# A graph-attention layer on one core: the order of a step, copies between lanes in place of matmuls, and early query blocks behind the table

## Chip, cores and metric

One Trainium2 chip, one of its cores. The metric is the device time of one execution in microseconds, as the median of several runs; lower is better. A profile holds one execution, with its span from the first to the last instruction. Engines: PE (matrix multiply, with PEld for its weight loads), DVE (vector), ACT (scalar functions), POOL (here: indirect loads), SP (issues loads and stores). Each works through its own queue in order, and waits on semaphores for the others.

## What is computed

A graph-attention layer over 3125 nodes of 128 features (8 heads of 16) and 100,000 edges sorted by destination, each with one of 5 relations, followed by two layer norms. Cut to what matters:

```python
for r in range(R):                                  # 5 relations
    mask = edge_types == r
    q = einsum('eh,khd->ekd', x[dst], W_Q[r])
    k = einsum('eh,khd->ekd', x[src], W_K[r])
    v = einsum('eh,khd->ekd', x[src], W_V[r])
    logits = (q * k).sum(-1) / scale + attn_bias[r]
    max_v = segment_max(where(mask, logits, NEG), dst)
    exp_l = where(mask, exp(logits - max_v[dst]), 0)
    attn = exp_l / (segment_sum(exp_l, dst)[dst] + 1e-12)
    out = out + segment_sum(attn * v, dst)
h = out.reshape(n, 128) @ out_proj_w.T + out_proj_b + x
y = (h - mean(h)) / sqrt(var(h) + eps) * ln_gamma + ln_beta
result = layernorm(x + y)
```

## The kernel before

**Start.** Inputs are loaded; W_K, W_V and W_Q are turned on PE (`wp`). A loop over 25 blocks of 128 nodes (`turn`, `table`, L318 to L341) turns a block of x, multiplies it with all W_K and W_V and stores the product to `kv_d` in DRAM: a table with one row of k and v for each node and relation. Beside it DVE makes keys, masks and indices (`side`). Then ACT issues the loads of beta, gamma, out_w, the bias (`floor`) and out_b (`lift`), and the pools of this stage (`load`, `pps`, `work`) are closed; their memory goes to the main pools (`ps`, `flow`, and the kv tiles 3 to 5).

**Queries.** A block of queries (`turn_q`, `turned`, `queries`, `first_part`, `remainder`, `second_part`, `third_part`, `store_q`) is x times W_Q, split into three bf16 parts whose sum is the f32 value, and stored to `q_d` in DRAM. `queries` makes it in two halves, of 3 and 2 relations. Blocks 0 to 3 are made before the main loop, each with its own load of x; the others inside it: `q_from` gives the step at which block b begins (q0); its second half follows one step later (q1), its last part and its store another step later (q2).

**Main loop.** The edges are cut into 196 groups of 512, and a step k has three groups: 66 steps, and a few more to drain. Each step issues, in an order written out by hand (the tile framework keeps this order on each engine), pieces of several groups of three:
- `fetch(k+3)` on SP: edge keys `kt`, query rows `qw`, masks `mk`. `gather` on POOL, up to three steps ahead: 12 indirect loads of table rows to one of six `kv` buffers.
- `spot(k+2)` on DVE and `spread_q(k+1)` on PE: the query of each edge (`qe`, in PSUM).
- `logits(k)` on DVE (three instructions, L632 to L635); `turn_logits` on PE, to lanes: one partition for each of group, relation and head, 120 in all, 512 edges along it; `keep_logits` on ACT.
- `scans(k)` on DVE: a running maximum forward and one back, restarted where the destination changes. So each lane has the maximum of every destination within its group of 512. A destination may straddle two groups: `joins` brings each lane the last value of the lane 40 before it, and the first value of the lane 40 behind it (40 lanes to a group; over the border of a step from and to the neighbouring step's tile `m`). Before, this is a product with a shifted unit matrix on PE, from `shift`, to a PSUM tile `c`; it runs for step k-1, as it needs m of step k.
- `less_max(k-2)` on DVE takes c into account and subtracts the maximum; `exps(k-2)` on ACT; `turn_exps(k-2)` on PE turns back; `weights(k-2)` (ACT) and `weigh(k-2)` (DVE) multiply with v. `weigh` is the last reader of a kv buffer.
- `places` (k-2) on ACT: a one-hot matrix for each group; `sums` (k-3) on PE adds up by destination; `carry` (ACT) hands a group's last destination to the next group.
- `norm(k-3)`, `relations(k-3)`, `by_node(k-4)`: division, sum over relations, copy to `oT`.
- For a block whose edges are all done (`done_at`): `project` on PE, one step later `residual` (DVE) and `norms` (a square root on ACT, then DVE), two steps after that `store_z`.

Of the kernel before, what the change touches and what calls it, by code (L numbers as in the profile page):

```python
# [8 lines left out]
F32 = mybir.dt.float32  # L9
BF16 = mybir.dt.bfloat16  # L10
# [107 lines left out]
def windowed_path(  # L118
# [15 lines left out]
    def keep(name, shape, dt=F32):  # L134
        return const.tile(shape, dt, name=name)
# [24 lines left out]
    work = pre.enter_context(tc.tile_pool(name="work", bufs=2))  # L160


    full = (NT - 1) * P
    xn = load.tile([P, NT, H], F32, name="xn")
    nc.vector.memset(xn[:, NT - 1, :], 0.0)
# [56 lines left out]
    base = load.tile([HG, 2], I32, name="base")  # L222


    ident = keep("ident", [P, P])
    make_identity(nc, ident)

    def iota(name, pattern, n, base=0, mult=0, dt=F32, pool=const):
        t = pool.tile([P, n], dt, name=name)
        nc.gpsimd.iota(  # L230
            t, pattern=pattern, base=base, channel_multiplier=mult,
            allow_small_or_imprecise_dtypes=True,
        )
        return t
# [4 lines left out]
    relf = iota("relf", [[1, R]], R, pool=load)  # L239
    nrel = iota("nrel", [[-1, R]], R, pool=load)  # L240
    lane = iota("lane", [[LANES, G3], [HEADS, R], [1, HEADS]], L3, mult=-1, pool=load)
    far = iota("far", [[1, 8 * LANES]], 8 * LANES, base=-L3, mult=-1, pool=load)
    eps_t = keep("eps_t", [P, 1])
    nc.vector.memset(eps_t, LN_EPS)
    ones = keep("ones", [P, P])
# [58 lines left out]
            op=ALU.is_equal,  # L304
        )

    shift = keep("shift", [P, 8 * LANES])
    gather_heads = keep("gather_heads", [P, G3, HEADS])

    def lanes():  # L310
        nc.vector.tensor_scalar(shift, far, 0.0, None, op0=ALU.is_equal)
        nc.vector.tensor_scalar(lane, lane, 0.0, None, op0=ALU.is_equal)
        nc.vector.tensor_reduce(
            gather_heads, lane.rearrange("p (i r k) -> p i k r", r=R, k=HEADS), AX.X, ALU.add
        )
# [163 lines left out]
    for b in range(NT):  # L479
# [3 lines left out]
        for f in side.get(b, ()):  # L483
            f()


    nc.scalar.dma_start(beta_t, beta.partition_broadcast(P))
    nc.scalar.dma_start(gamma_t, gamma.partition_broadcast(P))
# [20 lines left out]
    def groups(k):  # L509
        return range(k * G3, min(NGR, (k + 1) * G3)) if 0 <= k < NST else ()  # L510
# [45 lines left out]
    def first_part(b, c0):  # L556
        pr, q3, n = live["pr", b, c0]
        nc.scalar.copy(q3[:, :, 0, :], pr)
# [112 lines left out]

    def joins(k):
        n = len(groups(k)) * LANES
        c = ps.tile([L3, 2], F32, name="c", tag="small")
        m = live["m", k]
        left = [(m[:n, GE - 1 : GE], shift[:n, 2 * LANES : 2 * LANES + n])]
        if k:
            p = live["m", k - 1]
            left.append((p[:, GE - 1 : GE], shift[:L3, 5 * LANES : 5 * LANES + n]))
        right = [(m[:n, 0:1], shift[:n, 4 * LANES : 4 * LANES + n])]  # L680
        if k + 1 < NST:
            a, an = live["m", k + 1], len(groups(k + 1)) * LANES
            right.append((a[:an, 0:1], shift[:an, LANES : LANES + n]))
        for s, parts in enumerate((left, right)):
            for j, (col, w) in enumerate(parts):
                nc.tensor.matmul(  # L686
                    c[:n, s : s + 1], w, col, start=(j == 0), stop=(j == len(parts) - 1)
                )
        live["c", k] = c

    def less_max(k):
        n = len(groups(k)) * LANES
# [115 lines left out]
    def residual(b):  # L808
# [8 lines left out]
        moments(live["mv", b][:, 0, :], h[:n], n)  # L817
        live["h", b] = h

    def norms(b):  # L820
        mv = live.pop(("mv", b))
        sd = flow.tile([P, 2], F32, name="sd")
        nc.scalar.activation(sd, mv[:, :, 1], AF.Sqrt, bias=eps_t, scale=1.0)  # L823
        nc.vector.reciprocal(sd, sd)
        if b < NT:
            n = min(P, N - b * P)
            h = live.pop(("h", b))
            nc.vector.scalar_tensor_tensor(
                h[:n], h[:n], mv[:n, 0, 0:1], gamma_t[:n], op0=ALU.subtract, op1=ALU.mult
            )  # L830
            y = flow.tile([P, H], F32, name="y")
            nc.vector.scalar_tensor_tensor(
                y[:n], h[:n], sd[:n, 0:1], live.pop(("xr", b))[:n], op0=ALU.mult, op1=ALU.add
            )
            if ("mv", b + 1) not in live:
                live["mv", b + 1] = pair()
# [19 lines left out]
    for b in range(1, NT):  # L856
        done_at[b] = max(done_at[b], done_at[b - 1] + 1)
    done_at[NT] = done_at[NT - 1] + 1


    q_from = []
    for b in range(NT):
        need = min(g for g in range(NGR) if min(block_of(g) + 1, NT - 1) >= b) // G3
        q_from.append(need - 6)
    for b in range(NT - 2, -1, -1):
        if q_from[b + 1] > 0:
            q_from[b] = min(q_from[b], q_from[b + 1] - 2)

    first_b = [b for b in range(NT) if q_from[b] < 1]
    gathered = -1  # L870
    for gathered in range(KVA):
        gather(gathered)
    for b in first_b:
        fetch_x("xq", b)
        turn_q(b)
        turned(b)
        for c0, c1 in ((0, RH), (RH, R)):
            queries(b, c0, c1)
            first_part(b, c0)
            remainder(b, c0)  # L880
            second_part(b, c0)
            third_part(b, c0)
        store_q(b)
    for k in range(3):
        fetch(k)
    spot(0)
    spread_q(0)
    spot(1)
    for k in range(done_at[NT] + 3):
        q0 = next((b for b in range(NT) if q_from[b] == k and b not in first_b), None)  # L890
        q1 = next((b for b in range(NT) if q_from[b] == k - 1 and b not in first_b), None)
        q2 = next((b for b in range(NT) if q_from[b] == k - 2 and b not in first_b), None)

        if k + 3 < NST:
            fetch(k + 3)
        for b in range(NT):
            if q_from[b] == k + 1 and b not in first_b:
                fetch_x("xq", b)
            if done_at[b] == k:
                fetch_x("xr", b)  # L900
            if done_at[b + 1] + 2 == k:
                store_z(b)
# [5 lines left out]
        for b in range(NT):  # L908
            if done_at[b] + 1 == k:
                residual(b)  # L910
        if groups(k - 2):
            less_max(k - 2)
            exps(k - 2)
        if groups(k - 4):
            by_node(k - 4)
        if q0 is not None:
            turn_q(q0)
            turned(q0)
        if q1 is not None:
            queries(q1, RH, R)  # L920
            first_part(q1, RH)
        if q2 is not None:
            third_part(q2, RH)
            store_q(q2)

        sum_g = list(groups(k - 3))
        place_g = list(groups(k - 2))

        def sum_next():
            if sum_g:  # L930
                g = sum_g.pop(0)
                sums(g)
                carry(g)

        def place_next():
            if place_g:
                places(place_g.pop(0))

        sum_next()
        if groups(k):  # L940
            logits(k)
        if groups(k - 2):
            turn_exps(k - 2)
            weights(k - 2)
            place_next()
        sum_next()
        if q0 is not None:
            queries(q0, 0, RH)
            first_part(q0, 0)
        if groups(k):  # L950
            turn_logits(k)
            keep_logits(k)
        place_next()
        if groups(k - 2):
            weigh(k - 2)
        sum_next()
        place_next()
        if groups(k + 2):
            spot(k + 2)
        if groups(k + 1):  # L960
            spread_q(k + 1)
        if q0 is not None:
            remainder(q0, 0)
            second_part(q0, 0)
            third_part(q0, 0)
        if q1 is not None:
            remainder(q1, RH)
            second_part(q1, RH)
        if groups(k):
            scans(k)  # L970
        if groups(k - 1):
            joins(k - 1)
            live.pop(("m", k - 2), None)
        if groups(k - 3):
            norm(k - 3)
            relations(k - 3)
        for b in range(NT):
            if done_at[b] == k:
                project(b)
        for b in range(NT + 1):  # L980
            if done_at[b] + 1 == k:
                norms(b)

    ctx.close()

# [504 lines left out]
```

## Time and profile before

| | us |
|---|---|
| median of 3 runs | 1239.91 (1233.91 to 1240.34) |
| the profiled execution, its time | 1239.47 |
| its span | 1237.7 |
| start: table of k and v, up to the first gather | 0 to 93.1 |
| four query blocks, first fetches, up to the first `prod` | 93.1 to 148.3 |
| steps, up to the last gather | 148.3 to 1145.2 |
| the rest | 1145.2 to 1237.7 |
| PE busy | 977.8 |
| DVE busy | 875.6 |
| POOL busy | 802.4 |
| ACT busy | 651.8 |

Busy time counts an engine's instructions, not the issue time before a DMA. In a line of the list of instruction groups, out<-in names the tiles, xN counts the instructions; behind the bar stand their busy time, the mean of one in ns, and the idle time of the engine just before them with what ended it. In the list of waits, "A x <- B y: t, n, m" says that engine A, before the instruction that writes x, waited for B's y, t us in total, n times, m at the longest. In the timeline the first number is the start, the second the duration.

### The profile page before, as it was taken

The page shows a single profiled execution, that of the slowest core. Times are in us where ns is not written, and L with a number is a line of the kernel's source. Part 1 is how long each engine was busy: PE and PEld are TensorE (multiplying, and loading weights), DVE is VectorE, ACT ScalarE, POOL GpSimd, SP SyncE. Part 2 cuts the span into 40 slices and gives each one's busy share as a digit, 9 for nine tenths or more (in the row PEclk, how much of TensorE's full clock was granted, in tenths as well). Part 3 has the DMA queues.
Part 4 walks back from the last instruction along what each step waited for, and adds up shares of the span by engine and source line. Part 5 has one row for each costly group of instructions (what it writes and reads, how often), then busy time and mean ns, then how long its engine had stood idle before and what let it go on. Part 6 is the DMA issues. An engine that isn't in the chain of part 4 may idle for free.

```text
span 1237.7 us, 19625 instructions
## 1 busy us (share of the span) xinstructions
PE 977.8 (79%) x6463; PEld 787.2 (64%) x6463; DVE 875.6 (71%) x1366; ACT 651.8 (53%) x1828; POOL 802.4 (65%) x857
## 2 busy tenths in 40 slices
PE   5963268797879787878878787887887877888985
PEld 3531267676667676767767676776676766777763
DVE  4771287786778677768777777867776867798843
ACT  2421035475566474556556446656555655676662
POOL 4007777777777777777777677767767677777000
PEclk9995577777777687776777677868677778787865
DMA  7654775555555465555556555546555555555000
GB/s 186 270 208 138 224 225 158 173 174 162 170 171 173 142 186 160 177 157 167 158 161 183 152 157 173 170 132 189 154 161 160 163 153 176 166 164 142 12 1 13
DMA packets 108507, 196.78 MB, mean 159 GB/s; under 512 B 21614, under 2 KB 67947, under 8 KB 108276
## 3 DMA queue, kind: packets, MB, share of 16 engines
q0 software_dynamic: 37952, 102.82, 28.9%
q1 hardware_dynamic: 65934, 88.45, 21.6%
q10 hardware_dynamic: 4510, 4.17, 1.4%
q8 instruction: 53, 0.87, 0.3%
q14 instruction: 58, 0.48, 0.1%
HBM read 164.95 MB, written 30.40 MB: 158 GB/s over the span
## 4 chain that ended last, share of the span: by engine, by line
PE 48%; ACT 22%; DVE 18%; issue 4%; POOL 4%; DMA 3%; ACTq 1%; DVEq 0%; SPq 0%
PE both L754 16%; ACT at L737 8%; PE ex L714 6%; ACT at L740 4%; PE prq L553 4%; PE both L751 4%; PE pr L331 4%; PE lt L647 4%; POOL kv L527 4%; PE both L783 3%; PE qe L615 3%; ACT L823 2%; DVE m L667 2%; DVE m L663 2%; DVE ls L700 2%
## 5 line engine op out<-in xcount | busy, mean ns | idle before, releaser
L527 POOL DMA_INDIRECT kv<-kv_d,idx x784 | 789.9, 1008 | 335.4 <-issue 227.9
L754 PE MATMUL both<-wv,at 128*125 128x136 f32 x1568 | 370.9, 374 | 4.3 <-ACT pt L762 3.4
L754 PEld LDWEIGHTS both<-wv,at 128*125 128x125 f32 x1568 | 294.6, 255 | 77.3 <-issue 64.8
L737 ACT ACTIVATE at<-row_at,nkey 128x125 f32<-128x125 f32 x784 | 248.3, 391 | 0.0
L707 ACT ACTIVATE ls<-ls 120x512 f32<-120x512 f32 x66 | 41.6, 630 | 253.5 <-DVE ls L700 253.5
L615 PE MATMUL qe<-qw,hot 125*128 125x128 bf16 x2352 | 150.6, 226 | 9.0 <-DMA qw<-q_d 9.0
L714 PE MATMUL ex<-gather_heads,ls 120*128 120x24 f32 (+1 forms) x528 | 99.8, 335 | 72.4 <-ACT ls L707 71.0
L615 PEld LDWEIGHTS <-hot 125*128 125x128 bf16 x2352 | 145.7, 102 | 11.2 <-DVE hot L603 9.4
L714 PEld LDWEIGHTS ex<-gather_heads,ls 120*128 120x128 f32 (+1 forms) x528 | 97.6, 275 | 80.2 <-ACT ls L707 80.1
L686 PE MATMUL c<-m,shift 120*120 120x1 f32 (+1 forms) x524 | 69.5, 247 | 74.8 <-DVE m L667 74.8
L729 DVE TENSOR_TENSOR wv<-kv,ex 128x1536 f32<-128x1536 f32 x66 | 114.3, 1732 | 15.0 <-ACT wv L723 15.0
L740 ACT ACTIVATE at<-at 128x500 f32<-128x500 f32 x196 | 121.5, 620 | 6.2
L633 DVE TENSOR_REDUCE lg<-prod 128x96 f32<-128x1536 f32 x66 | 114.6, 1736 | 2.3
L686 PEld LDWEIGHTS c<-m,shift 120*120 120x120 f32 (+1 forms) x524 | 65.3, 192 | 77.1 <-DVE m L667 76.9
L632 DVE TENSOR_TENSOR prod<-kv,qe 128x1536 f32<-128x1536 f32 x66 | 114.2, 1730 | 0.0
L663 DVE TENSOR_TENSOR_SCAN m<-mk,lt 120x512 f32<-120x512 bf16 x66 | 80.2, 1216 | 26.6 <-ACT ls L656 25.9
L751 PE MATMUL both<-pt,over 125*5 125x136 f32 x390 | 96.4, 338 | 0.0
L762 ACT COPY pt<-both 125x136 f32<-125x136 f32 x195 | 52.3, 268 | 60.7 <-PE both L754 60.3
L667 DVE TENSOR_TENSOR_SCAN m<-mk,m 120x512 f32<-120x512 bf16 x66 | 80.8, 1224 | 2.3
L572 DVE TENSOR_TENSOR q<-rem,q 128x384 bf16<-128x384 f32 (+1 forms) x50 | 24.5, 490 | 81.7 <-ACT q L568 81.7
L783 PE MATMUL both<-rsum,o 125*128 125x25 f32 x392 | 67.9, 310 | 16.8 <-DVE o L772 15.2
L783 PEld LDWEIGHTS both<-rsum,o 125*128 125x128 f32 x392 | 62.5, 237 | 19.3 <-issue 14.1
(150 smaller groups left out, 1038.9 us busy)
## 6 DMA issues: line engine op xcount, KB each, us to landing
kt<-key_d SPq DMA_DIRECT2D x65, 384.0 KB
qw<-q_d SPq DMA_DIRECT2D x196, 96.0 KB
kv_d<-kvs SPq DMA_DIRECT2D x24, 640.0 KB
kv<-kv_d,idx POOLq DMA_INDIRECT x784
q_d<-q SPq DMA_DIRECT2D x25, 480.0 KB
mk<-msk_d SPq DMA_DIRECT2D x196, 50.1 KB
xq<-in_x SPq DMA_DIRECT2D x24, 64.0 KB
xr<-in_x SPq DMA_DIRECT2D x24, 64.0 KB
```

What stands on the lines that cost most here:

```text
L527: nc.gpsimd.indirect_dma_start(out=kv[:, t, i, :], out_offset=None, in_=kv_d[:, :], in_offset=bass.IndirectOffsetOnAxis(ap=idx[:, t, g : g ...
L615: nc.tensor.matmul(qe[:, t, i, :], hot[:, i, t * P : (t + 1) * P], qw[:WR, i, s, :], start=(s == 0), stop=(s == 2),)
L632: nc.vector.tensor_tensor(prod, flat(kv[:, :, :, :H], n), flat(qe, n), op=ALU.mult)
L633: nc.vector.tensor_reduce(lg, heads(prod), AX.X, ALU.add)
L686: nc.tensor.matmul(c[:n, s : s + 1], w, col, start=(j == 0), stop=(j == len(parts) - 1))
L714: nc.tensor.matmul(ex[:, t], ls[: n * LANES, t * P : (t + 1) * P], gather_heads[: n * LANES, :n], start=True, stop=True,)
L729: nc.vector.tensor_tensor(heads(flat(wv[:, :, :, :H], n)), heads(flat(kv[:, :, :, H:], n)), flat(ex, n)[:, :, :, None].to_broadcast([P, n ...
L737: nc.scalar.activation(at[:, t, :], row_at[:, :WR], AF.Abs, bias=nkey[:, t, g : g + 1], scale=1.0)
L740: nc.scalar.activation(at, at, AF.Relu, bias=1.0, scale=-1.0)
L751: nc.tensor.matmul(pp[:R], over[:WR, g, :], live.pop(("pt", g - 1)), start=False, stop=False)
L754: nc.tensor.matmul(pp[:WR], at[:, t, :], wv[:, t, i, :], start=(t == 0), stop=(t == T - 1))
L783: nc.tensor.matmul(both[:, i, PW:], o5[:, i], rsum[:WR], start=True, stop=True)
```

## The change

The joins' matmuls become SP copies between SBUF tiles; the order within a step is redone (`norms` is split, its square root goes to `roots`); query blocks 0 to 3 are made behind the table in the pools of the start, from the x that lies there; `ident` is made first. The diff, cut to its core:

```diff
+    ident = keep("ident", [P, P])
+    make_identity(nc, ident)
     full = (NT - 1) * P
     xn = load.tile([P, NT, H], F32, name="xn")
...
-    ident = keep("ident", [P, P])
-    make_identity(nc, ident)
...
-    far = iota("far", [[1, 8 * LANES]], 8 * LANES, base=-L3, mult=-1, pool=load)
...
-    shift = keep("shift", [P, 8 * LANES])
...
-        nc.vector.tensor_scalar(shift, far, 0.0, None, op0=ALU.is_equal)
...
+    first_q = 4
+    tps, xts, prs = [], [], []
+    for b in range(first_q):
+        tp = pps.tile([P, P], F32, name="tp", tag="tr", bufs=2)
+        nc.tensor.transpose(tp, xn[:, b, :], ident)
+        xt = work.tile([P, P], F32, name="xT", bufs=4)
+        nc.scalar.copy(xt, tp)
+        q3 = work.tile([P, R, 3, H], BF16, name="q3", bufs=3)
+        for c0, c1 in ((0, RH), (RH, R)):
+            n_ = c1 - c0
+            pr = pps.tile([P, 4, H], F32, name="pr", tag="pr", bufs=4)
+            nc.tensor.matmul(pr[:, :n_], xt, wq[:, c0:c1, :], start=True, stop=True)
+            nc.scalar.copy(q3[:, c0:c1, 0, :], pr[:, :n_])
+            rem = work.tile([P, RH, H], F32, name="rem", bufs=2)
+            nc.vector.tensor_tensor(
+                rem[:, :n_], pr[:, :n_], q3[:, c0:c1, 0, :], op=ALU.subtract
+            )
+            nc.scalar.copy(q3[:, c0:c1, 1, :], rem[:, :n_])
+            nc.vector.tensor_tensor(
+                q3[:, c0:c1, 2, :], rem[:, :n_], q3[:, c0:c1, 1, :], op=ALU.subtract
+            )
+        nc.sync.dma_start(
+            q_d[b * P * R : (b + 1) * P * R, :].rearrange("(p r) c -> p (r c)", r=R),
+            q3.rearrange("p r s h -> p (r s h)"),
+        )
+
     nc.scalar.dma_start(beta_t, beta.partition_broadcast(P))
     nc.scalar.dma_start(gamma_t, gamma.partition_broadcast(P))
...
     def joins(k):
         n = len(groups(k)) * LANES
-        c = ps.tile([L3, 2], F32, name="c", tag="small")
         m = live["m", k]
-        left = [(m[:n, GE - 1 : GE], shift[:n, 2 * LANES : 2 * LANES + n])]
-        if k:
-            p = live["m", k - 1]
-            left.append((p[:, GE - 1 : GE], shift[:L3, 5 * LANES : 5 * LANES + n]))
-        right = [(m[:n, 0:1], shift[:n, 4 * LANES : 4 * LANES + n])]
-        if k + 1 < NST:
-            a, an = live["m", k + 1], len(groups(k + 1)) * LANES
-            right.append((a[:an, 0:1], shift[:an, LANES : LANES + n]))
-        for s, parts in enumerate((left, right)):
-            for j, (col, w) in enumerate(parts):
-                nc.tensor.matmul(
-                    c[:n, s : s + 1], w, col, start=(j == 0), stop=(j == len(parts) - 1)
-                )
+        c = flow.tile([L3, 2], F32, name="c", bufs=4)
         live["c", k] = c
+        with nc.allow_non_contiguous_dma(reason="one element of each lane"):
+            if k == 0:
+                nc.vector.memset(c, 0.0)
+            else:
+                p, q = live["m", k - 1], live["c", k - 1]
+                nc.sync.dma_start(c[:LANES, 0:1], p[2 * LANES :, GE - 1 : GE])
+                nc.sync.dma_start(q[2 * LANES :, 1:2], m[:LANES, 0:1])
+            if n > LANES:
+                nc.sync.dma_start(c[LANES:, 0:1], m[: 2 * LANES, GE - 1 : GE])
+                nc.sync.dma_start(c[: 2 * LANES, 1:2], m[LANES:, 0:1])
+            else:
+                nc.vector.memset(c[:, 1:2], 0.0)
...
+    def roots(b):
+        sd = flow.tile([P, 2], F32, name="sd")
+        nc.scalar.activation(sd, live["mv", b][:, :, 1], AF.Sqrt, bias=eps_t, scale=1.0)
+        live["sd", b] = sd
+
     def norms(b):
-        mv = live.pop(("mv", b))
-        sd = flow.tile([P, 2], F32, name="sd")
-        nc.scalar.activation(sd, mv[:, :, 1], AF.Sqrt, bias=eps_t, scale=1.0)
+        sd, mv = live.pop(("sd", b)), live.pop(("mv", b))
         nc.vector.reciprocal(sd, sd)
```

The steps of blocks 4 and up in `q_from` stay as they were. The body of a step, before and after, in the order in which it is issued (conditions left out; `sum` stands for `sums` and `carry` of the next group of k-3, `place` for `places` of the next group of k-2; done, stats and rooted are the blocks with `done_at` = k, k-1 and k-2):

```text
before                                    after
fetch(k+3), xq, xr, store_z               fetch(k+3), xq, xr, store_z (one step later)
gather(k+3)                               gather(k+3)
residual(stats)                           residual(stats)
less_max(k-2), exps(k-2)                  by_node(k-4)
by_node(k-4)                              turn_q, turned (q0)
turn_q, turned (q0)                       third_part(q2, second half), store_q(q2)
queries, first_part (q1, second half)     third_part(q1, first half)
third_part(q2, second half), store_q(q2)  logits(k)
sum                                       place, sum, place, sum
logits(k)                                 less_max(k-2), exps(k-2)
turn_exps(k-2), weights(k-2)              turn_logits(k), keep_logits(k)
place, sum                                spot(k+2)
queries, first_part (q0, first half)      turn_exps(k-2)
turn_logits(k), keep_logits(k)            scans(k), joins(k)
place                                     place
weigh(k-2)                                weights(k-2), weigh(k-2)
sum, place                                sum
spot(k+2), spread_q(k+1)                  queries, first_part (q0, first half)
remainder, second_part, third_part (q0)   queries, first_part (q1, second half)
remainder, second_part (q1)               spread_q(k+1)
scans(k), joins(k-1)                      norm(k-3), relations(k-3)
norm(k-3), relations(k-3)                 remainder, second_part (q0), (q1)
project(done)                             norms(rooted), roots(stats)
norms(stats)                              project(done)
```

The loop before it that made blocks 0 to 3 goes; `fetch(0)` to `fetch(2)`, `spot(0)`, `spread_q(0)` and `spot(1)` stay in front of step 0.

More of the change, by code (lines that the diff above doesn't have):

```diff
@@ L858, in windowed_path @@
     done_at[NT] = done_at[NT - 1] + 1
-    q_from = []
-    for b in range(NT):
+    block_at = {k: b for b, k in done_at.items()}
+    q_from = {}
+    for b in range(first_q, NT):
         need = min(g for g in range(NGR) if min(block_of(g) + 1, NT - 1) >= b) // G3
[L864 to L869, printed above, removed]
+        q_from[b] = need - 6
+    for b in range(NT - 2, first_q - 1, -1):
+        q_from[b] = min(q_from[b], q_from[b + 1] - 2)
+    assert q_from[first_q] >= 0
+    q_at = {k: b for b, k in q_from.items()}
     gathered = -1
@@ L872, in windowed_path @@
         gather(gathered)
[L873 to L883, printed above, removed]
+    if 0 in q_at:
+        fetch_x("xq", q_at[0])
     for k in range(3):
@@ L888, in windowed_path @@
     spot(1)
[L889 to L892, printed above, removed]
+    for k in range(done_at[NT] + 4):
+        q0, q1, q2 = q_at.get(k), q_at.get(k - 1), q_at.get(k - 2)
+        done, stats, rooted = block_at.get(k), block_at.get(k - 1), block_at.get(k - 2)
         if k + 3 < NST:
             fetch(k + 3)
[L896 to L902, printed above, removed]
+        if k + 1 in q_at:
+            fetch_x("xq", q_at[k + 1])
+        if done is not None and done < NT:
+            fetch_x("xr", done)
+        if block_at.get(k - 3):
+            store_z(block_at[k - 3] - 1)
         while gathered + 1 < NST and gathered + 1 <= k + AHEAD:
@@ L906, in windowed_path @@
             gather(gathered)
[L908 to L924, printed above, removed]
         sum_g = list(groups(k - 3))
@@ L937, in place_next @@
                 places(place_g.pop(0))
-        sum_next()
+        if stats is not None and stats < NT:
+            residual(stats)
+        if groups(k - 4):
+            by_node(k - 4)
+        if q0 is not None:
+            turn_q(q0)
+            turned(q0)
+        if q2 is not None:
+            third_part(q2, RH)
+            store_q(q2)
+        if q1 is not None:
+            third_part(q1, 0)
         if groups(k):
             logits(k)
+        place_next()
+        sum_next()
+        place_next()
+        sum_next()
+        if groups(k - 2):
+            less_max(k - 2)
+            exps(k - 2)
+        if groups(k):
+            turn_logits(k)
+            keep_logits(k)
+        if groups(k + 2):
+            spot(k + 2)
         if groups(k - 2):
             turn_exps(k - 2)
+        if groups(k):
+            scans(k)
+            joins(k)
+            live.pop(("m", k - 2), None)
+        place_next()
+        if groups(k - 2):
             weights(k - 2)
-            place_next()
+            weigh(k - 2)
         sum_next()
@@ L949, in windowed_path @@
             first_part(q0, 0)
[L950 to L959, printed above, removed]
+        if q1 is not None:
+            queries(q1, RH, R)
+            first_part(q1, RH)
         if groups(k + 1):
             spread_q(k + 1)
+        if groups(k - 3):
+            norm(k - 3)
+            relations(k - 3)
         if q0 is not None:
@@ L964, in windowed_path @@
             second_part(q0, 0)
-            third_part(q0, 0)
         if q1 is not None:
@@ L968, in windowed_path @@
             second_part(q1, RH)
[L969 to L982, printed above, removed]
+        if rooted is not None:
+            norms(rooted)
+        if stats is not None:
+            roots(stats)
+        if done is not None and done < NT:
+            project(done)
     ctx.close()
```

## Prediction

> **What bounds the kernel now.** First the stretches, since start, steady run and end differ:
> ```profile
> core 0: us, PE busy (x) PEld busy (x) DVE busy (x) ACT busy (x) POOL busy (x), PEclk, DMA share, GB/s
> 260.00:660.00 400.00, 330.94 (x2307) 276.41 (x2308) 301.72 (x445) 228.75 (x656) 305.85 (x303) 0.76 0.56 167
> 660.00:1060.00 400.00, 330.02 (x2295) 275.14 (x2294) 298.25 (x449) 228.74 (x648) 290.92 (x291) 0.76 0.54 161
> 1145.20:1212.00 66.80, 59.01 (x356) 47.73 (x355) 42.61 (x75) 43.10 (x122) 0.03 (x1) 0.70 0.03 8
> ```
> No engine is full in the steady run (PE 83%, DVE 75%), and POOL looks the same at 73 to 76%. But a gather's issue time is not counted as busy, so I read the gathers by themselves, from the list by line and from the tile's view:
> ```profile
> L527 POOL DMA_INDIRECT kv<-kv_d,idx x784 | 789.9, 1008 | 335.4 <-issue 227.9 <-DMA floor<-in_L_gnn_attn_bias 73.1 <-DVE wv L729 27.6
> ...
> L527 POOL DMA_INDIRECT kv<-kv_d,idx x784: 942/946/1869, 93.1 to 1144.0; - x196
> ...
>   issue: 227.9, 748
> ```
> A gather takes 1.008 us and 227.9/748 = 0.305 us of issue: 1.313 us, so 15.75 us for the twelve of a step. POOL never idles for anything else but 73.1 us before the first and some 34 us in all behind them, 27.6 of it for kv buffers that `weigh` (L729) has not released. So there are two pipelines of nearly one speed: POOL at 15.75 us a step, and everything else, whose pace is the distance of the `prod` rows (L632). That pace is (1069.7 - 243.5)/50 = 16.5 us from step 7 to 57; a step without block work takes 12.4 (707.5 to 720.0), its neighbours 16.9 and 18.7. Third, the waits:
> ```profile
> DVE q L572 <- ACT q L568: 81.7, 29, 4.6
> PE c L686 <- DVE m L667: 74.8, 24, 5.5
> PE ex L714 <- ACT ls L707: 71.0, 31, 3.3
> DVE h L816 <- PE pj L797: 56.0, 24, 2.8
> DVE sd L824 <- ACT sd L823: 50.0, 25, 2.3
> ```
> All five fall in steps with block work (24 to 31 times each): there the in-order queues wait for each other in a ring. Fourth, the two ends of the timeline:
> ```profile
> 93.10 1.04 POOL L527 DMA_INDIRECT kv<-kv_d,idx  x1 [73.13 <-DMA floor<-in_L_gnn_attn_bias]
> ...
> 103.67 0.43 SPq L538 DMA_DIRECT2D xq<-in_x  x1
> ...
> 135.74 0.43 SPq L585 DMA_DIRECT2D kt<-key_d  x1
> ...
> 148.31 1.73 DVE L632 TENSOR_TENSOR prod<-kv,qe 128x1536 f32<-128x1536 f32 x1
> ...
> 1144.04 1.19 POOL L527 DMA_INDIRECT kv<-kv_d,idx  x1 [0.30 <-issue]
> ...
> 1167.53 1.75 DVE L632 TENSOR_TENSOR prod<-kv,qe 128x1536 f32<-128x1536 f32 x1
> ```
> Step 0's gathers are issued by 107.9, its `prod` runs at 148.3: 40 us late, of which 42 us (93.4 to 135.7) are the four query blocks, made one behind the other. The lag is 22 us at step 6, grows to 46 us at step 34 (the six kv buffers are then full and POOL waits), and is 27.6 us at step 64. Gathers end at 1145.2, and 92.5 us follow.
>
> **The change, part by part.**
>
> *Joins.* Eight matmuls a step leave PE (68.4 us over 65 steps, 1.05 us each step), and with them PE's 74.8 us wait for the second scan. Four SP copies of 40 or 80 elements of 4 B come in. The nearest row is `floor` (L492: 40 x 4 B, three issues in 1.97 us, DVE goes on 1.5 us after the last): four cost 4 x 0.66 = 2.6 us of SP's queue and X = 4.1 us from scan to landing. The upper bound is the slowest small load, `dst_r`'s tail at the start (1.87 to 10.36): X = 8.5 us. I take 4.1, the form being the same. SP now stops at scans(k); behind it stand fetch(k+4) (1.5 steps or more before `spot`, nearly three before `spread_q`), xq and xr (a step early) and z: nobody waits. By q1's mean packet (21.6% x 16 x 1237.7/65,934 = 65 ns) 15,800 more packets are 64 us on each of 16 engines, 5% on top of a share of 0.55: at worst tenths of a us for a landing.
>
> *Order of a step.* I walk a plain step from its first `prod`, by row means. DVE: logits 1.75 + 1.75 + 0.66 = 4.2; less_max 2 x 0.28 + 0.75, to 5.5; spot 0.65, to 6.1. ACT: exps 0.63 from 5.5, then keep_logits 0.59, to 6.8, for which the scans wait 0.7 (they start behind it in the trace). Scans 2.45, to 9.2. PE's `ex` (1.9 from 6.1) and ACT's third places (1.9) and weights (0.24) are done by 8.9, so weigh runs 9.2 to 11.0 and norm to 12.0. PE and ACT do by_node, two places and two sums while DVE is at the logits. Its PE rows fit: 661 us over 800/16.5 = 48.5 steps is 13.6, less 1.05 for the joins. Block work on DVE is 1.95 (query parts) + 1.05 (residual) + 1.7 (norms) = 4.7 us each, 25 in 66 steps: 1.8 a step. third_part one step later, roots one step before norms and project behind roots take the three DVE waits above off its queue: they were 188 us. So the compute pace is about 12.0 + 1.8 = 13.8, bounds 12.4 (the plain step) and 16.5 (nothing gained). At 13.8 it is under POOL's 15.75, and the bound passes to POOL. Two us of waits a step would still be covered.
>
> *Early query blocks.* Their loads of x go (xn is there), and PE, ACT and DVE make them behind the table. The chain per block, ACT's copy of xT 0.27, PE 1.2, casts 0.48 + 0.51 + 0.37 + 0.40, DVE rem 0.56 + 0.42 between them, and hand-overs, is about 4.9 us (bounds 3.3 by ACT and DVE overlapped, 10.5 as now); four from 88.5 end at 108. The beta to lift loads then follow on ACT's queue (3.9 us), the main pools open at 113, and fetch(0) to `prod` takes 148.3 - 135.7 = 12.6: logits(0) at 126. With the early steps' pace (44.8 us for four) logits(4) is at 171; gather 4 ends at 169.2. From there POOL leads. Whether the blocks take 3.3 or 6 us does not move the end; at 10.5 step 4 would be 22 us late, made up at 2 us a step.
>
> *ident first* frees PE's 12.3 us wait for it, but the table still starts behind ACT's wp copies (16.88 to 18.15), for ACT issues loads until 15.55: nothing, bound 1 us. *shift* and *far* go: 0.3 us of DVE and 0.4 of POOL, hidden.
>
> *The sum.* Gathers start at 93.1, since they wait for the last kv_d store (issued at 88.5), which nothing delays. 784 x 1.313 = 1029: they end at 1122 instead of 1145.2. Gather 64 is over 4 x 1.31 = 5.3 us earlier and lands 2.7 us later (the chain's first kv landing): logits(64) at 1119.5, against 1167.5. From there the trace takes 1237.7 - 1167.5 = 70.2 us. In the last steps without logits two sums and two carries now stand ahead of exps, which by my walk costs 2 us: 72. Span 1119.5 + 72 = 1191.5; with 1.8 us around it (1239.47 less 1237.7; that run is 0.4 under the median 1239.91) **1193 us**. Bounds of the terms: gather 1.305 (the mean of 660 to 1060) -6, tail -8 or +6, start -1 or +2.
>
> [...]
>
> **Rivals.**
> 1. The compute pace stays as it was (16.24 from step 4 to 64), since the ring of waits only moves. For: ACT's exps now queue behind two places and two carries, which wait for PE. Against: the plain step of 12.4 us. 171.4 + 60 x 16.24 + 72 + 1.8 = 1219.
> 2. The first gather waits for the main pools: the page names `floor`'s landing as what ended its 73.1 us, and that load moves 20 us back. Against: L527 uses early tiles only. 1193 + 20 = 1213.
> [...]
> 4. **Slower: the copies land late.** less_max(k-1), at 4.2 of step k+1, needs what joins(k) sends at 9.2 of step k: a period of at least X + 5.0. It passes POOL's 15.75 at X = 10.7, and the old total + 0.5% (16.7 a step) from X = 11.7. No row shows that (4.1, 8.5), but SP waits long on other things (257.5 us on L563). At X = 12.5: 171.4 + 60 x 17.5 + 74 = 1295.
> 5. No change: rival 1 with a pace of 16.6: 171.4 + 996 + 74 = 1241.
>
> **Chances.** Forecast 0.66, rivals in order 0.13, 0.07, 0.03, 0.06, 0.05. A measurement of this kernel tells about 0.5% (6 us) from no change. Faster 0.88 (forecast and rivals 1 to 3, less a little of 1), same 0.05, slower 0.07. The forecast's own range is 1180 to 1206; taking in rivals 1 to 3 gives 1178 to 1224, with 4 and 5 and the forecast's thin lower end left out.
>
> **What would show it.** `prod` rows 15.7 us apart from step 5 on, with DVE idle before them for a kv landing, and POOL without its wait for `weigh`; first gather near 93, first `prod` near 126; last gather near 1122, some 70 us before the end; L686 gone; less_max without a wait for c. Wrong if `prod` rows stand over 15.9 apart with full kv buffers, if the first gather starts after 100, or if DVE waits for c's copies.

## The result, and the profile after

The kernel after took 1198.66 us, median of 4 runs (1191.58 to 1201.0); the kernel before 1238.49 beside it. The ratio is 0.967, 95% interval 0.962 to 0.972: faster. Ratios, here and below, are taken over undisturbed executions alone, so they can differ a little from the quotient of the medians beside them. The profiled execution took 1198.12 us, its span 1196.3. The prediction was 1193.

The stretches of the kernel after (columns as before: length, busy time of each engine, granted clock, DMA share, GB/s):

```profile
260.00:660.00 400.00, 319.21 (x2208) 254.01 (x2207) 316.64 (x471) 242.78 (x682) 306.38 (x308) 0.79 0.58 170
660.00:1060.00 400.00, 317.19 (x2249) 255.19 (x2247) 317.22 (x476) 246.41 (x691) 306.98 (x306) 0.80 0.58 172
1131.20:1196.30 65.10, 44.59 (x161) 32.33 (x161) 23.18 (x67) 25.10 (x71) 0.00 (x0) 0.50 0.03 8
```

DVE now does 317 us of work in 400 in place of 302 and 298, so more steps pass in the same time. The end has a clock of 0.50.

What POOL waited for in the kernel after (sum in us, times, longest):

```profile
POOL kv L549 <- issue: 222.6, 730, 0.3
POOL kv L549 <- DVE rem L497: 75.8, 1, 75.8
POOL kv L549 <- DMA kv<-kv_d,idx: 5.2, 17, 0.3
```

The 26.5 us that POOL waited for `weigh` between 260 and 1060 are gone; what is left are gaps of 0.3 us, its own issue time under other names. POOL gathers without a stop from its first to its last. The ends of that run, and the last two steps:

```profile
94.78 1.28 POOL L549 DMA_INDIRECT kv<-kv_d,idx  x1 [75.79 <-DVE rem L497]
...
1116.45 1.75 DVE L654 TENSOR_TENSOR prod<-kv,qe 128x1536 f32<-128x1536 f32 x1 [2.25 <-PE qe L637]
...
1117.17 0.95 POOL L549 DMA_INDIRECT kv<-kv_d,idx  x1 [0.30 <-issue]
...
1131.19 0.68 DVE L654 TENSOR_TENSOR prod<-kv,qe 128x512 f32<-128x512 f32 x1
```

So (1118.1 - 94.8)/784 = 1.305 us for a gather, 15.66 for a step. The first `prod` comes at 125.4 (148.3 before). From step 2 to 64 each `prod` starts 2 to 8 us behind the end of its step's last gather (22 to 47 us before), and from step 7 to 58 the `prod` rows are 15.67 us apart (16.48 before). The waits of the other engines:

```profile
PE both L775 <- ACT pt L783: 92.5, 65, 2.7
...
DVE m L685 <- ACT ls L678: 81.5, 66, 5.0
...
PE ex L735 <- ACT ls L728: 70.2, 64, 2.3
...
ACT q L590 <- DVE rem L585: 46.1, 41, 2.6
...
DVE h L837 <- PE pj L818: 43.9, 25, 3.4
...
DVE prod L654 <- DMA kv<-kv_d,idx: 31.0, 16, 4.3
...
DVE prod L654 <- PE qe L637: 20.0, 16, 2.3
...
DVE q L594 <- ACT q L590: 8.6, 18, 0.6
```

The wait for the joins (L686) has gone. DVE's wait for the query parts has shrunk from 81.7 to 8.6 us, and ACT now waits 46.1 us for their remainder (4.4 before). DVE waits for a kv landing in 16 steps of 66, and a short wait of PE and DVE comes back in every step.

### The profile page after: what moved, and what is told of

Its sections match the earlier page's. It is cut to its first block, busy times and chain, and to the rows that moved or that the text cites. A ratio compares the mean times of both kernels' runs of the same rounds, so it can differ in the third digit from the quotient of the medians.

```text
span 1196.3 us, 18904 instructions
## 1 busy us (share of the span) xinstructions
PE 918.8 (77%) x5939; PEld 712.9 (60%) x5939; DVE 879.3 (73%) x1367; ACT 657.1 (55%) x1828; POOL 796.8 (67%) x856
## 4 chain that ended last, share of the span: by engine, by line
POOL 25%; PE 24%; DVE 18%; issue 12%; ACT 12%; DMA 7%; ACTq 0%; SPq 0%; DVEq 0%; POOLq 0%
POOL kv L549 25%; PE both L775 6%; DMA kv<-kv_d,idx 6%; PE qe L637 4%; PE pr L327 4%; PE ex L735 4%; DVE lg L655 3%; DVE prod L654 3%; ACT at L758 3%; ACT ls L728 2%; ACT at L761 2%; DVE wv L750 2%; DVE m L685 2%; DVE m L689 2%; DVE ls L721 2%
## 5 line engine op out<-in xcount | busy, mean ns | idle before, releaser
L775 PE MATMUL both<-wv,at 128*125 128x136 f32 x1568 | 347.4, 354 | 92.5 <-ACT pt L783 92.5
L775 PEld LDWEIGHTS both<-wv,at 128*125 128x125 f32 x1568 | 258.4, 228 | 169.0 <-ACT pt L783 106.1
L637 PEld LDWEIGHTS <-hot 125*128 125x128 bf16 x2352 | 194.3, 122 | 28.8 <-issue 24.2
L637 PE MATMUL qe<-qw,hot 125*128 125x128 bf16 x2352 | 196.8, 261 | 5.3 <-DMA kv<-kv_d,idx 5.3
L735 PE MATMUL ex<-gather_heads,ls 120*128 120x24 f32 (+1 forms) x528 | 102.9, 341 | 70.3 <-ACT ls L728 70.2
L810 ACT COPY oT<-both 128x25 f32 x196 | 35.5, 181 | 151.5 <-PE both L804 69.4
L669 PE MATMUL lt<-ident,lx 128*120 128x128 f32 (+1 forms) x264 | 53.9, 342 | 52.5 <-DVE lx L657 52.4
L669 PEld LDWEIGHTS lt<-ident,lx 128*120 128x120 f32 (+1 forms) x264 | 38.0, 169 | 59.2 <-issue 45.2
L804 PE MATMUL both<-rsum,o 125*128 125x25 f32 x392 | 55.4, 274 | 10.9 <-DVE o L793 10.9
L327 PE MATMUL pr<-wkv,xT 128*128 128x512 f32 x150 | 62.9, 564 | 0.7 <-ACT wkv L277 0.4
```

The lines of the kernel that those rows point to most:

```text
L327: nc.tensor.matmul(pr[:, : c1 - c0, :], xT, wf[:, c0:c1, :], start=True, stop=True)
L637: nc.tensor.matmul(qe[:, t, i, :], hot[:, i, t * P : (t + 1) * P], qw[:WR, i, s, :], start=(s == 0), stop=(s == 2),)
L735: nc.tensor.matmul(ex[:, t], ls[: n * LANES, t * P : (t + 1) * P], gather_heads[: n * LANES, :n], start=True, stop=True,)
L775: nc.tensor.matmul(pp[:WR], at[:, t, :], wv[:, t, i, :], start=(t == 0), stop=(t == T - 1))
```

## The experiments

They ran later, on four chips, and on each of them the kernel before itself took 1695 to 1771 us, not 1239. Times are therefore given as a ratio to the kernel before on the same chip. Why everything is slower there became the question, since it turns the sign of the change. The last column is worked out from the timeline rows: from the end of the last matmul of the relations to `by_node` on ACT, median over the steps in which ACT stood idle by then (fewer than five such steps: -).

| run | us | before, same chip | ratio, 95% | `prod` to `prod`, step 7 to 58 | relations to `by_node` |
|---|---|---|---|---|---|
| after, first comparison | 1198.7 | 1238.5 | 0.967 [0.962, 0.972] | 15.7 | 0.04 |
| early blocks alone | 1701.9 | 1694.7 | 1.005 [1.001, 1.010] | 23.4 | - |
| copies alone | 1655.1 | 1694.7 | 0.975 [0.967, 0.984] | 22.5 | - |
| both, old order | 1643.9 | 1694.7 | 0.968 [0.959, 0.976] | 22.3 | - |
| after, no early blocks | 1941.5 | 1694.7 | 1.141 [1.127, 1.155] | 26.9 | 9.1 |
| after, joins as matmuls | 2058.5 | 1704.5 | 1.209 [1.198, 1.219] | 29.0 | 9.5 |
| after, copies late | 2020.2 | 1704.5 | 1.167, one run | 28.5 | 13.2 |
| before, 9 gathers | 1530.6 | 1704.5 | 0.898 [0.889, 0.908] | 20.7 | - |
| after, 9 gathers | 1731.9 | 1704.5 | 1.016 [1.005, 1.028] | 23.6 | 8.3 |
| after, again | 1991.8 | 1770.6 | 1.119 [1.106, 1.131] | 28.0 | 12.3 |
| after, 12 matmuls for qe | 1767.2 | 1770.6 | 0.996 [0.992, 0.999] | 24.6 | under 1 |
| after, users later | 1915.7 | 1703.7 | 1.124 [1.100, 1.149] | 26.7 | - |
| after, qe early, filled end | 1777.0 | 1703.7 | 1.048 [1.036, 1.061] | 24.8 | under 1 |

**1. Parts of the change alone.** Early blocks alone (before, with the added loop behind the table and without the old one):

> The kernel before with the four early query blocks made behind the table, order and joins as before. Theory (before is bound by the pace of its compute steps, after by the gathers): the first prod comes 22 us earlier, at about 125, but the steps keep 16.2 to 16.5 us, so gathers wait for kv buffers more than before and the time is 1214 to 1222 us. Rival (the start is all that counts; the order of a step is worth nothing): the steps run at the gathers' 15.7 us and the time is 1195 to 1203 us. Rival (the start is hidden by the lead of the gathers): 1235 to 1240 us.

Copies alone (before, with the new `joins`, called for step k behind its scans):

> The kernel before with the joins as four small SP copies behind the scans of their step, and nothing else changed. Theory: PE loses 1.05 us of matmuls and its wait for the second scan, but less_max now stands only 1 to 4 us behind the scan whose copies it needs, against about 4 us until they land, so DVE waits 1 to 3 us a step there and the pace is hardly better or a little worse: 1230 to 1260 us. Rival (taking the joins off PE breaks the ring by itself): 15.7 us a step from the middle on, 1205 to 1220 us.

Both together in the old order:

> The kernel before with both the early query blocks and the joins as copies, the order of a step as before: what is left to the kernel after is the order alone. Theory: some 20 us under the run with copies alone, 1210 to 1240 us, and 12 to 40 us above the kernel after. Rival (order worth nothing once the joins are copies): 1196 to 1204 us.

And the kernel after with the early blocks back in their old place:

> The kernel after with its first four query blocks made where they were before, one behind the other ahead of the first step. Theory: gathers start at about 94 all the same, the first prod comes at about 148, some 23 us later than in the kernel after, and the compute steps, which can run faster than the 15.65 us of the gathers, make up that lag in 10 to 20 steps: 1196 to 1204 us. Rival (compute can't run faster than the gathers, or the early blocks are worth their 22 us): the lag stays and the time is 1215 to 1222 us.

No expected time holds, for the base is another. As ratios: early blocks bring nothing, copies 2.5%, and the new order costs 17%: on one chip, copies with the old order are at 0.975 and with the new order at 1.141, both without early blocks. With copies alone DVE waits for c as expected, but 17.5 us in 12 steps and not 1 to 3 us in each. What the copies can save shows in the run with early blocks alone: there DVE waits 172.8 us, in 25 steps, on "remote" ahead of less_max (L722), the reader of the joins' product; with the copies beside them that line is gone. That early blocks bring nothing has its row in the start of the kernel after, run again (below):

```profile
183.24 0.95 POOL L549 DMA_INDIRECT kv<-kv_d,idx  x1 [0.30 <-issue]
...
192.06 1.75 DVE L654 TENSOR_TENSOR prod<-kv,qe 128x1536 f32<-128x1536 f32 x1 [55.56 <-remote]
```

Its qe ends at 130.0, but the first `prod` starts 8 us after POOL paused (at 184.2, with six buffers full). It is the same with and without early blocks: 191.8 with them alone, 194.2 without. "remote" stands where no release is on record.

**2. Joins, copies, gathers.** Joins as matmuls again:

```diff
-            joins(k)
...
+        if groups(k - 1):
+            joins(k - 1)
```

> The kernel after with the joins of step k-1 as matmuls again, placed behind the last sum of step k (where the scans of step k are long done), c in PSUM as before. Theory: PE gets 1.05 us more in a step of 15.65 us in which it is busy for about 12.5, so the gathers still set the pace: 1196 to 1206 us. Rival (the copies are what frees the ring): back to 16.2 us a step or more, 1225 to 1245 us.

Copies made late, by twelve more ahead of them:

```diff
+                for j in range(6 if n > LANES else 0):
+                    nc.sync.dma_start(spare[:LANES, 0, j : j + 1], p[2 * LANES :, GE - 1 : GE])
+                    nc.sync.dma_start(spare[LANES:, 1, j : j + 1], m[: 2 * LANES, 0:1])
```

> The kernel after with twelve more copies of 40 or 80 elements, to a spare tile, ahead of the four of each step on the same queue; by the four rows of the kernel after (0.56 to 0.83 us each) they make the four land about 8.4 us later, X about 12.5 us behind the scan in place of about 4. Theory (by the prediction's rival of late copies, less_max of the next step reads what joins sends, a period of X + 5.0): 17.5 us a step, some 1290 us, and less_max waits for c. Rival (less_max of step k-2 needs copies that are a whole step old, so that there is about 10 us more room): the time stays at 1196 to 1204 us and nobody waits for c.

Fewer gathers, in the kernel before and in the kernel after:

```diff
-            for t in range(T):
+            for t in range(T if k < KVB else T - 1):
```

> The kernel before, gathering from step 6 on only 9 of the 12 tiles of a step (the fourth slice keeps what the buffer held, so the output differs). Theory (the compute steps bound it): POOL needs only 11.8 us a step, the prod rows stay 16 to 16.5 us apart and the time stays at 1220 to 1240 us. Rival (the gathers bound both kernels): about 60 x 3.9 = 235 us less, or what the compute allows.

> The kernel after, gathering from step 6 on only 9 of the 12 tiles of a step (the fourth slice keeps what the buffer held, so the output differs). Theory (gathers bound it at 15.65 us a step, the compute steps could do about 13.8): the prod rows come 13.8 us apart and the time falls to 1075 to 1100 us. Rival (compute is at its own bound of about 15.6 too): 1185 to 1200 us.

The joins as matmuls cost more than the kernel after (1.209 against 1.119, on different chips). The late copies tell nothing of the rival: a step there takes 28.5 us, so a period of 17.5 can't bound it. DVE does begin to wait there for c, a little (it never did in the kernel after):

```profile
DVE m L721 <- DMA c<-m: 14.1, 5, 4.3
```

With a quarter of the gathers gone both kernels gain about 10% (0.898 of before; 1.016 against 1.119), though POOL waited 610.3 us for `weigh` in the kernel after run again, and so didn't bound it. Under these conditions it is the gathers that slow the compute steps down; the compute pace of the first comparison could not be had from these two.

**3. Where the time stands.** The kernel after, unchanged, and with qe made from one bf16 part of three:

```diff
-                for s in range(3):
+                for s in range(1):
...
-                        start=(s == 0), stop=(s == 2),
+                        start=(s == 0), stop=(s == 0),
```

> The kernel after, unchanged, as the reference for the eight runs before it, in which the kernel before took 1695 to 1704 us, 37% over its time in the first comparison, and PE's releases reached ACT and DVE 4 to 13 us after the last matmul of qe and of the relations (0.04 us between relations and by_node in the first trace of this kernel). If the kernel before takes about 1239 us here, the first comparison repeats: 1190 to 1202 us. If it takes about 1700 us: theory (what makes the time there is how often a queue stands still for a late release of PE, and the new order has by_node ahead of a step's sums): between the runs without early blocks and with 9 gathers, 1740 to 1950 us, with prod rows lagging their gathers far more than 8 us and POOL waiting for weigh. Rival (the longer times are those of the changed parts alone): about 0.967 of the kernel before, 1640 us.

> The kernel after with qe made from the first of the three bf16 parts of q alone: 12 matmuls and 12 weight loads a step ahead of the relations in place of 36 and 36 (the other two parts are left out, which lowers the accuracy of q). If the kernel before takes about 1239 us here (gathers bound the kernel after): no change, 1185 to 1202 us. If it takes about 1700 us: theory (releases of PE come late by what a dense run of matmuls has piled up) the delay from the relations to by_node falls from 8 to 13 us to under 5, and the time by 250 to 450 us under the kernel after of the same chip. Rival (each release is late by a fixed time): within 3% of it.

First the waits of the kernel after run again, then one step of it by time:

```profile
PE both L775 <- ACT pt L783: 696.2, 57, 15.3
POOL kv L549 <- DVE wv L750: 610.3, 45, 37.5
ACT oT L810 <- remote: 547.9, 40, 17.0
...
DVE prod L654 <- remote: 250.3, 30, 55.6
DVE h L837 <- remote: 238.9, 17, 15.5
```

```profile
1021.38 1.73 DVE L750 TENSOR_TENSOR wv<-kv,ex 128x1536 f32<-128x1536 f32 x1
...
1023.38 0.95 POOL L549 DMA_INDIRECT kv<-kv_d,idx  x1 [15.86 <-DVE wv L750]
...
1024.33 2.79 PE L637 MATMUL qe<-qw,hot 125*128 125x128 bf16 x36
...
1025.08 0.56 DVE L585 TENSOR_TENSOR rem<-prq,q 128x384 f32<-128x384 f32 x1 [0.38 <-ACT q L580]
...
1025.67 0.51 ACT L590 CAST q<-rem 128x384 bf16<-128x384 f32 x1 [0.62 <-DVE rem L585]
...
1026.95 0.80 PE L804 MATMUL both<-rsum,o 125*128 125x25 f32 x6
...
1032.07 1.75 DVE L654 TENSOR_TENSOR prod<-kv,qe 128x1536 f32<-128x1536 f32 x1 [4.48 <-remote]
...
1037.50 1.34 POOL L549 DMA_INDIRECT kv<-kv_d,idx  x1 [0.30 <-issue]
1038.59 0.18 ACT L810 COPY oT<-both 128x25 f32 x1 [12.40 <-issue]
```

`weigh` frees a buffer, and POOL starts a burst of gathers. Inside the burst PE issues qe and the relations. They end at 1027.1 and 1027.8 by their rows, yet `prod` goes on at 1032.1 and `by_node` at 1038.6, with nothing ahead of them on their engines. The same place in the first comparison's trace, with POOL gathering all the time too:

```profile
704.36 3.19 PE L637 MATMUL qe<-qw,hot 125*128 125x128 bf16 x36
...
707.39 0.80 PE L804 MATMUL both<-rsum,o 125*128 125x25 f32 x6
...
708.29 1.75 DVE L654 TENSOR_TENSOR prod<-kv,qe 128x1536 f32<-128x1536 f32 x1 [0.60 <-PE both L804]
...
708.75 0.38 ACT L810 COPY oT<-both 128x25 f32 x2
```

There the users follow in under a microsecond. Over all waits of `prod`, `by_node` and `h` for PE in the kernel after run again: where PE's last matmul ended outside a burst, the user followed in 0.04 us (median of 12); inside one, in 10.9 us (of 100), and this grows with the number of PE instructions since the burst began (correlation 0.88). DVE's releases are not late in the burst shown: `rem` ends at 1025.64 and ACT's cast of it starts at 1025.67. With 12 matmuls for qe the median inside a burst falls to under 1 us, the first `prod` comes at 138.2, and the kernel is 11% faster. The drop is some 217 us (0.123 of 1770.6), under the 250 to 450 that the theory gave: ACT now waits 462.6 us on "remote" ahead of `pt` (110.4 before). Part of it may be PE's lighter work, which this run doesn't tell apart; the next two take no work away.

**4. Order again.** Two edits of the order alone test this without taking work away. The users of PE's last matmuls moved down the step:

```diff
-        if stats is not None and stats < NT:
-            residual(stats)
-        if groups(k - 4):
-            by_node(k - 4)
...
             keep_logits(k)
+        if groups(k - 4):
+            by_node(k - 4)
         if groups(k + 2):
             spot(k + 2)
+        if stats is not None and stats < NT:
+            residual(stats)
```

> The kernel after with by_node and residual, the users of the last matmuls of the step before, moved from the head of a step behind keep_logits and spot (later by about two sums on ACT, by the logits and less_max on DVE). Theory (in these runs a release of PE that falls into a burst of gathers reaches ACT and DVE 8 to 13 us late, and standing at the head of the in-order queues it holds up the whole step): the 590 us that ACT waits ahead of by_node and the 240 us that DVE waits for pj shrink to under 200 together, some of it comes back at the next waits (pt, prod), and the ratio to the kernel before falls from 1.12 to 0.95 to 1.05. Rival (the whole of PE's work is late in a burst, whoever waits for it first): the wait moves to pt and prod and the ratio stays at 1.09 to 1.15.

And qe ahead of `weigh`, out of the burst, with the end filled (`filler` is called between the two first sums with n = 2, ahead of `less_max` with 3 and behind `norm` with 5):

```diff
             turn_exps(k - 2)
+        if groups(k + 1):
+            spread_q(k + 1)
...
-        if groups(k + 1):
-            spread_q(k + 1)
...
+    def filler(k, n):
+        if k >= NST - 2:
+            t = ps.tile([L3, GE], F32, name="lt")
+            for _ in range(n):
+                nc.tensor.matmul(t, spare[:, :L3], spare, start=True, stop=True)
```

> The kernel after with two edits. First, qe of the next step is made right behind turn_exps, ahead of weigh, in place of behind it: theory (weigh frees a kv buffer and so starts a burst of gathers; what PE issues in the burst decides how late its releases are: 78 to 89 instructions 8 to 13 us, 39 instructions 0.7 us): the 72 instructions of qe leave the burst, prod no longer waits for a late release, by_node waits 0.5 to 4 us in place of 12, and the ratio to the kernel before falls from 1.12 to 0.93 to 1.02. Rival (the delay is tied to the time since weigh and not to PE's instructions in the burst): 1.08 to 1.14. Second, from step 64 on ten spare bf16 matmuls of 512 columns a step on zeros fill PE's gaps (they write a PSUM tile that nobody reads). From the prod of step 65 to the end the kernel after took 65.1 us at a clock of 0.50 with PE busy for 44.6. Theory (the gaps let the clock fall, and that is the 8 us by which the tail was longer than predicted): clock 0.7 or more there, six matmuls of a sum in 1.0 to 1.3 us in place of 1.70, and 54 to 61 us. Rival (the clock has fallen for another reason, or spare work costs what it brings): clock 0.50 to 0.55 and 65 to 72 us.

Moving the users is the rival's case: 1.124, and the wait goes to the next user, the copy `pt` behind the sums:

```profile
ACT pt L783 <- remote: 532.1, 56, 15.8
...
DVE prod L654 <- remote: 337.6, 35, 57.2
```

Moving qe is the theory's case in kind, though not in full size: 1.048, `by_node` under 1 us behind the relations (median), `prod` waiting on "remote" once (the first, 56.2 us), but `pt` for 422.1 us. So in these runs the lateness is PE's, inside a burst, and it belongs to what PE issues there, whoever comes first to wait for it.

The filled end, from the `prod` of step 65 on (columns as in the stretches above):

```profile
1744.90:1802.60 57.70, 43.63 (x219) 27.92 (x217) 22.85 (x67) 24.30 (x70) 0.00 (x0) 0.88 0.03 9
```

The same stretch took 65.1 us at a clock of 0.50 in the kernel after, in the first comparison and when run again. With spare matmuls among PE's work the clock is 0.88, six matmuls of a sum take mostly 0.96 us in place of 1.70, and the stretch is 7.4 us shorter. Not all of it is gain: the spare matmuls begin in step 64, which takes 17.4 us in place of 14.7 (qe ahead of `weigh` stands there too). From the `prod` of step 64 to the end it is 75.1 us against 79.8, 4.7 us less. So the clock at the end depends on what PE is given to do. What in it decides (the length of its gaps, their share of the time, or the kind of its matmuls) is not shown: up to the last matmul the longest wait in PE's rows is 2.31 us unfilled, and 2.06 us is still there in the filled end.

## Why the prediction was right, and where it was off

**The bound passes to POOL: right, but closely.** POOL has no stop, `prod` rows 15.67 us apart, full buffers never. Rival 1 and 5 fall with that. The compute pace was put at 13.8; DVE waited for a landing 31 us in 16 steps, so compute ran only some 31/66 = 0.5 us a step ahead of POOL, at about 15.2 (an estimate from these rows), inside the bounds of 12.4 and 16.5. That is a margin of half a microsecond where about 2 were forecast, so the passing of the bound came near to luck. The walk through a plain step gave 12.0. The step 64 to 65 has hardly a gather beside it, but it is no plain step in the kernel after:

```profile
1122.21 1.28 ACT L728 ACT_TABLE_LOAD   x1
...
1129.71 0.15 DVE L848 RECIPROCAL sd<-sd 128x2 f32<-128x2 f32 x1
...
1130.96 0.32 DVE L868 TENSOR_SCALAR z<-y,mv,sd 128x128 f32<-128x128 f32 x1
```

It holds the `norms` of a block, 1.5 us of DVE up to the next `prod`, and ahead of `exps` the load of ACT's function table after a square root, 1.28 us. The new order puts `norms` one step later; in the kernel before the same work stands ahead of the `prod` of step 64 (1167.53), and the step behind it has no block work:

```profile
1166.11 0.31 DVE L844 TENSOR_SCALAR z<-y,mv,sd 128x128 f32<-128x128 f32 x1
...
1178.33 0.68 DVE L632 TENSOR_TENSOR prod<-kv,qe 128x512 f32<-128x512 f32 x1
```

So 14.7 after (in both runs) and 10.8 before are not the same work. Less 1.3 and 1.5, the step after is at about 11.9, an estimate, and the walk's 12.0 is not refuted. What was then put too low is the block work: 1.8 us a step forecast, some 3.2 between 12.0 and 15.2. It counted DVE alone; the 23 table loads ahead of `exps` are 29.5 us, 0.45 a step, on ACT. How the rest divides is not shown.

**Gathers.** Start 94.8 against 93.1 (bound +2), 1.305 us against 1.313 (bound -6); last end 1118.1 against 1122. `prod` of step 64 at 1116.5 against 1119.5. Rival 2 falls: the label on the first gather's wait changed (L497, the remainder of an early block, in place of `floor`), its end hardly did.

**Early blocks.** First `prod` at 125.4 against 126.

**Joins.** Of the four copies, three stand behind the scan; with their median issue times (0.765 + 0.561 + 0.592) and 1.70 us to land (from the chain of the run with 9 gathers) X is about 3.6, against 4.1. Nobody waits for c. Rival 4 did not happen; its period was not tested.

**The clock in the steps** rose from 0.76 to 0.79 and 0.80; steps made slower by a falling clock, third among the chances at 0.03, did not come. In the 800 us from 260 to 1060, 3 of PE's waits are above 2.5 us (35 before); whether the clock rose for that is not shown.

**The tail is the term that was mis-sized:** 72 us predicted from the `prod` of step 64 to the end, 79.8 measured (70.2 before). Step 64 to 65 takes 3.9 us more (14.7 against 10.8). Some 2.8 of them, by the estimate above, are the `norms` and the table load that the new order moves behind the last gather; the walk had put nothing for that. The copies may have a part in the rest: with the old order and copies this step takes 12.5 and 12.0. From the `prod` of step 65 on it is 65.1 us against 59.4, at a clock of 0.50 against 0.54; with spare matmuls it was 57.7 at 0.88, so the clock has a part in these 5.7 us; how large a part, beside the new order's, is not shown. The prediction had counted instructions (2 us) at the clock of before. With -3 from the gathers the sum is 1193 - 3 + 8 = 1198.

**What the prediction had no rival for** is the other condition of the machine. With releases of PE late inside a burst of gathers (10.9 us, median), the order that puts qe, relations and projection right behind `weigh` is 11.9% slower than before. No row of the first two traces shows it. How the first comparison's 3.3% divides between early blocks, copies and order is not settled: no part was run under its conditions. Why releases are late there is open too. The trace of the kernel after run again holds 10,365 records of releases, that of the first comparison 27,554, with about as many instructions. Inside bursts all twelve later traces hold only 3.7 to 5.1 such records per us, where the first two hold 22 and 25 while POOL gathers. Whether the late releases and the lower number of records belong together no run shows.

## What to carry to other kernels

When two pipelines of nearly one speed meet, measure the new bound's margin as well as the old one's: here half a microsecond a step decides. Behind an instruction that frees a buffer can come a burst of transfers, as the gathers behind `weigh` here; keep what others wait for out of PE's dense run in that burst, or put it ahead, for where releases are late (here 8 to 13 us) the order decides over more than the work. When an order moves work to a later step, look where it lands at the end: here `norms` landed behind the last gather. And a drain in which PE is not kept busy can be paid at a lower clock: here it was 0.50, with PE busy for 44.6 of 65.1 us, and 0.88 with spare matmuls, which gave 4.7 us back, net.

## What the runs showed of the hardware

- In the later runs the user of PE's result followed 0.04 us after PE outside a burst of gathers, 10.9 us inside one (medians of the kernel after run again), and under 1 us inside one with 24 fewer matmuls of qe.
- SP's issues beside back-to-back gathers were slow at the start of the kernel after run again: three qw loads took 11.90 us to issue at 163.6, 3.17 us at 191.6 with POOL paused, and 2.83 us at 1032.1 inside a burst; in the first comparison, with POOL gathering, they took 2.05 us at 115.7.
- PE's clock was 0.50 at the end of the kernel after with PE busy for 44.6 of 65.1 us, and 0.88 with spare matmuls among its work, though a wait of 2.06 us remained.
